# A two-layer decoder on one core: loading the tokens first, clearing the expert slots from another DMA queue, and writing out the first sequence's combination between the last shared groups

## The chip, the cores and the metric

The kernel runs on one core of a Trainium2 chip. A core has five engines, each with its own in-order instruction queue: TensorE (PE, matrix products and transposes[...]), VectorE (DVE), ScalarE (ACT), GpSimd (POOL) and SyncE (SP, which here only issues DMAs). [...] The metric is the device time of one execution in microseconds (us). Times of single instructions come from one profiled execution, and they are counted from the start of its span.

## What is computed

A decoder of two layers runs over 16 sequences of 256 tokens with 128 features, all in float32, with a context of 64 tokens of 96 features for each sequence. After each of six sublayers the input is added and the rows are normalised (post-norm). Cut to its frame, the reference is:

```python
x = _layernorm(x + _L0_attn_ref(x, ...))            # causal, 16 heads of 8
x = _layernorm(x + _L0_xattn_ref(x, ctx_768, ...))  # 8 heads of 16 on the context
x = _layernorm(x + _L0_ffn_ref(x, ...))             # 64 experts, top 6, and a shared FFN
x = _layernorm(x + _L1_attn_ref(x, ...))            # causal, 16 heads of 64
x = _layernorm(x + _L1_xattn_ref(x, ctx_768, ...))  # 16 heads of 64 on the context
x = _layernorm(x + _L1_ffn_ref(x, ...))             # attention whose tokens use 128, 64, 32 or 16 features
```

In the expert sublayer each token picks six of 64 experts by its softmax scores and a bias. An expert takes the first 64 tokens that picked it (tokens in order), each in a slot of its own; later ones are dropped. The expert and the shared FFN are both `silu(x w1) * (x w3)` times `w2`, with 88 hidden features in an expert and 176 in the shared FFN. A token's result is the sum of its experts' rows, each times its score, plus the shared FFN's row.

## The kernel before

**Recording and orders.** Most of the work is written as streams. A `Recorder` stands in for the engines: while a stream's function runs, calls are only stored, as units per engine. `interleaved` then takes an order, a long string written out ahead of time, in which each character names a stream and an engine, and emits the next unit of that stream on that engine:

```python
for c in order:
    b, e = divmod(LETTERS.index(c), len(ENGINES))
    for trace in waiting[b][e].pop(0):
        trace()
```

The sections under `manual_schedule` keep the emitted order on PE, DVE, ACT and POOL (`MANUAL`, L30). SP isn't in that set; the scheduler places SP's DMAs by when their buffers come free and what they depend on. Because all recorded calls pass through the helper at L141, nearly every row of the profile carries L141, and tile names tell the rows apart.

**Layer 0** (`ORDER0`, 17 streams). Stream 0, `contexts`, starts with `clear_slots` (L688 to 694): SP writes zeros over all 4096 slots of `xb` in DRAM (2 MB) and the spare row of `yb`. Then come the context's keys and values for layer 0 (`k0x`, `v0x`, from `ctxT`, `l0x_wk` and `l0x_wv`), and the products that fold layer 1's cross-attention into two tables in DRAM, `gd` and `hd`, one part for each head. The other 16 streams are `layer0(b)`, one for each sequence: load `x`, transpose it (`tp_x`), self-attention (tiles `..._0a`), norm, cross-attention (`..._0x`; the norm's inverse root `rs_0x` is a POOL instruction), norm into `x2` and, transposed, `x2T`, and the router. The router takes softmax scores (`sc`), adds the bias (`sb`), chooses six (`chosen`), counts slots with small products (`pos`), and gets each slot and each weight by comparing (`key`, `hit`). For each token tile and each of its six picks, POOL issues an indirect DMA that scatters 128 rows of `x2` into `xb`; there are 192 of these "puts".

**Experts** (program order). SP loads the weights of eight experts at a time (`e` tiles: `w1T`, `w3T`, `w2T`, 352 KB each, four groups in flight) and the constants of layer 1 (`l1_wqkv` 1.5 MB, `l1_wout`, and so on). The `e` tiles use memory that the pools of layer 0 release. `expert_tokens(g)` loads group g's 512 slots after all puts; PE transposes them (`xet`, `xeT`), then come the hidden products `eh`, `he`, the output `yp`, its copy `ye` on ACT, and SP's store to `yb`. The shared FFN runs in eight groups of 512 tokens: `shared_hidden(g)` makes `sh` on PE and `hs` on ACT and DVE, and `shared_out(g)` makes `z` on PE and adds it to `x2` on DVE. Groups 0 to 3 stand before the experts, groups 4 to 7 after them. `widths` prepares constants of the last sublayer in the middle of the experts.

**Layer 1** (`ORDER1`, 16 streams). First the pools of the experts are closed and new ones opened (`v1`, `vz`, `v2`); two tiles `vaf` are zeroed on POOL; and the value bias is folded into the output bias: DVE copies `bv`, PE multiplies it with `l1_wout` (`bv_out`), DVE adds the product to `l1_bout` (named `l_bout` in the profile; digits are left out of names). Each `layer1(b)` begins with 12 indirect DMAs on POOL that gather the tokens' expert rows `ge` from `yb`, and 12 DVE instructions that add them, weighted, to `x2` (`xr`). Then come norm (`st_0f`, `mv_0f`, `rs_0f`, result `x`), the transposed `x3T`, the products `qk` and `vp`, the output bias (`xpb_1a`, POOL), self-attention (`s_1a`, `nm_1a`, `p_1a`, `ptp_1a`), cross-attention with the tables `gx` and `hx` (loaded by SP from `gd` and `hd`), and the last sublayer.

## Time and profile before

| quantity | value |
|---|---|
| median of 3 runs (lowest to highest) | 1684.59 us (1684.14 to 1687.62) |
| the profiled execution's own time | 1679.19 us |
| span of the profiled execution | 1677.4 us |
| mean granted TensorE clock | 0.959 of full |
| busy PE, DVE, ACT, POOL | 1496.5, 1244.2, 1108.6, 830.6 us |
| DMA traffic | 73.89 MB, mean 44 GB/s |
| chain that ended last, by engine | PE 52%, DVE 24%, ACT 11%, issue 6%, POOL 4%, DMA 2% |

The profiled execution was about 5 us faster than the median; 1.8 us of its time lie around the span. A row of the profile gives a start, a duration, the engine, the operation, the tile written, the tiles read, their shapes and, in brackets, how long the engine had been idle and what ended that idle time. "SPq" is a DMA's issue in SyncE's queue, and not its transfer. The slices divide the span into 40 equal parts and give each engine's busy share in tenths.

By stage: layer 0 runs from 0 to about 626 us, the experts from 631.5 (first `eh`) to 668, the last shared groups and the transition to about 740, and layer 1 to the end.

### The profile page before, as it was taken

To read this page: it belongs to the slowest core of one execution; us is meant where nothing else is said; L and a number is where in the kernel's file an instruction comes from. 1 tells how busy PE (TensorE), PEld (TensorE's weight loads), DVE (VectorE), ACT (ScalarE), POOL (GpSimd) and SP (SyncE) were. 2 spreads that over 40 slices of the span, in tenths; PEclk is the share of its full clock that TensorE was granted. 3 is DMA by queue.
4 is the path that set the end of the run, shared out by engine and by line. 5 is a ranking of instruction groups with operands and counts; after the bars stand their busy time and mean duration, and the time that the engine had idled before them with its cause. 6 is when DMAs were issued, how large, how long until landed. Compare 5 with 4: busy or idle time off the path is not lost.

```text
span 1677.4 us, 36931 instructions
## 1 busy us (share of the span) xinstructions
PE 1496.5 (89%) x12738; PEld 1080.5 (64%) x12738; DVE 1244.2 (74%) x3788; ACT 1108.6 (66%) x3811; POOL 830.6 (50%) x910
## 2 busy tenths in 40 slices
PE   7989988889987679688998999998999999999996
PEld 4655555556554338466776877686777677777774
DVE  5788888879887643355778878777786787788675
ACT  4776777757776312155576777677676767786766
POOL 2144445444435440456727656664564576564441
PEclk9999999989999778789999999999999999999999
DMA  4111111111100066474202233222322333220000
GB/s 142 60 41 34 60 32 33 42 48 55 47 13 1 1 172 190 52 105 48 23 14 34 40 41 44 23 36 14 48 41 31 30 43 42 36 23 4 5 1 11
DMA packets 117190, 73.89 MB, mean 44 GB/s; under 512 B 46555, under 2 KB 106808, under 8 KB 116877
## 3 DMA queue, kind: packets, MB, share of 16 engines
q1 hardware_dynamic: 104717, 58.55, 12.8%
q0 software_dynamic: 12288, 13.00, 10.6%
q8 instruction: 102, 1.67, 0.4%
q14 instruction: 83, 0.68, 0.1%
HBM read 48.05 MB, written 35.65 MB: 50 GB/s over the span
## 4 chain that ended last, share of the span: by engine, by line
PE 52%; DVE 24%; ACT 11%; issue 6%; POOL 4%; DMA 2%; another core or an unknown queue 1%; SPq 0%; POOLq 0%; DVEq 0%; ACTq 0%
PE s_1a L141 5%; PE qk L141 4%; PE o_1a L141 4%; ACT p_0a L141 4%; PE ptp_1a L141 3%; PE s_0a L141 3%; PE ptp_1f L141 3%; PE vp L141 3%; PE pj_1x L141 3%; PE pj_1a L141 2%; PE ptp_0a L141 2%; DVE nm_0a L141 2%; PE s_1x L141 2%; ACT p_1a L141 2%; DVE x L141 2%
## 5 line engine op out<-in xcount | busy, mean ns | idle before, releaser
L141 POOL DMA_INDIRECT xb<-x,slots x192 | 189.1, 985 | 263.9 <-DVE hit L141 212.6
L141 POOL TENSOR_TENSOR p_1a<-p_1a,ri_1a 128x512 f32<-128x512 f32 x192 | 197.3, 1039 | 104.5 <-DVE ri_1a L141 89.3
L141 ACT ACTIVATE p_1a<-s_1a,nm_1a 128x256 f32<-128x256 f32 (+1 forms) x512 | 210.9, 445 | 50.5 <-DVE nm_1a L141 41.7
L141 ACT ACTIVATE p_0a<-s_0a,nm_0a 128x256 f32<-128x256 f32 (+1 forms) x512 | 211.5, 451 | 35.2 <-DVE nm_0a L141 33.6
L141 POOL DMA_INDIRECT ge<-yb,slots x192 | 195.7, 1019 | 54.4 <-issue 51.9
L141 ACT COPY pT_1a<-ptp_1a 128x512 f32<-128x512 f32 x192 | 106.1, 618 | 63.1 <-PE ptp_1a L141 55.1
L141 DVE TENSOR_REDUCE nm_1a<-s_1a 128x2 f32<-128x512 f32 (+1 forms) x192 | 126.1, 673 | 21.4 <-PE s_1a L141 21.3
L141 DVE TENSOR_REDUCE nm_0a<-s_0a 128x2 f32<-128x512 f32 (+1 forms) x192 | 125.0, 682 | 11.8 <-PE s_0a L141 10.5
L141 PE MATMUL qk<-x3T,l_wqkv 128*128 128x256 f32 x512 | 126.9, 390 | 2.7 <-issue 1.4
L141 ACT ACTIVATE p_1f<-s_1f,nm_1f 128x256 f32<-128x256 f32 x256 | 119.0, 499 | 10.4 <-DVE nm_1f L141 9.3
L141 PE MATMUL ptp_0a<-ident,p_0a 128*128 128x128 f32 x768 | 112.1, 281 | 13.5 <-ACT p_0a L141 7.9
L141 ACT COPY pT_0a<-ptp_0a 128x512 f32<-128x512 f32 x192 | 106.4, 615 | 23.7 <-PE ptp_0a L141 18.6
L141 ACT ACTIVATION_READ_ACCUMULATOR p_0a<-s_0a,nm_0a 128x1 f32 x512 | 120.8, 236 | 0.0
L141 ACT ACTIVATION_READ_ACCUMULATOR p_1a<-s_1a,nm_1a 128x1 f32 x512 | 117.9, 230 | 0.0
L141 PEld LDWEIGHTS qk<-x3T,l_wqkv 128*128 128x128 f32 x512 | 95.8, 197 | 20.1 <-issue 7.7
L141 PEld LDWEIGHTS ptp_0a<-ident,p_0a 128*128 128x128 f32 x768 | 86.4, 143 | 34.0 <-ACT p_0a L141 20.6
L141 PE MATMUL ptp_1a<-ident,p_1a 128*128 128x128 f32 x768 | 101.1, 275 | 7.7 <-POOL p_1a L141 3.9
L141 PE MATMUL s_1a<-kT,qT 64*128 64x256 f32 (+1 forms) x1024 | 104.4, 342 | 3.3 <-issue 2.3
L141 POOL TENSOR_TENSOR p_1x<-p_1x,cri_1x 128x512 f32<-128x512 f32 x64 | 65.9, 1044 | 66.6 <-DVE cri_1x L141 41.9
L141 PE MATMUL o_1a<-pT_1a,v 128*64 128x128 f32 x1536 | 95.4, 276 | 3.0 <-ACT p_1a L141 1.2
L141 PEld LDWEIGHTS s_1a<-kT,qT 64*128 64x128 f32 x1024 | 81.5, 192 | 23.3 <-issue 11.4
L141 DVE SCALAR_TENSOR_TENSOR xr<-ge,slot_w,xr 128x128 f32<-128x128 f32 x160 | 61.2, 383 | 46.8 <-DMA ge<-yb,slots 42.7
(258 smaller groups left out, 3710.9 us busy)
## 6 DMA issues: line engine op xcount, KB each, us to landing
gd<-g1x_sb SPq DMA_DIRECT2D x32, 256.0 KB
hd<-h1x_sb SPq DMA_DIRECT2D x32, 256.0 KB
gx<-gd SPq DMA_DIRECT2D x16, 512.0 KB
hx<-hd SPq DMA_DIRECT2D x32, 256.0 KB
xb<-x,slots POOLq DMA_INDIRECT x192
ge<-yb,slots POOLq DMA_INDIRECT x192
e<-in_w1T SPq DMA_DIRECT2D x8, 352.0 KB
e<-in_w3T SPq DMA_DIRECT2D x8, 352.0 KB
```

The lines of the kernel that those rows point to most:

```text
L141: r = f(*[made(x) for x in a], **{n: made(x) for n, x in k.items()})
```

## The change

Seven things are changed. Sizes, arithmetic and the number of heavy instructions stay as they are.

1. At the start, the tokens of sequence 0 and `l0_wqkv` are loaded first, then `ctxT`, `l0x_wk`, `l0x_wv`, then the rest of layer 0's weights, and the shared FFN's weights last. The two DMAs of `clear_slots` are issued by ScalarE, right after `l0_wqkv`.
2. The pool `fw` (scratch of the router and of the folded tables) is closed at the end of layer 0 and no longer after the experts.
3. `ORDER0` is rewritten. Compared engine by engine, the two orders differ in local swaps; in the last part more of the puts stand ahead of the last sequence's `rs_0x`.
4. `vaf` moves to the pool `wc` and is zeroed on DVE within `widths`; `v2` is opened early, on the right side of memory.
5. `gathered`, `combine`, `value_bias` and `add_value_bias` are functions of their own, and all that follows layer 0 lies in one manually scheduled section.
6. Between the last shared groups, the order is written out: the gathers of sequence 0 after `expert_out(7)`, the bias product before `shared_out(6)`, and the two halves of sequence 0's combination before and after `shared_out(7)`.
7. `ORDER1` is rewritten; stream 0 lacks its gathers and sums.

Where the built programs stand against each other, SP's order changes as well, although no line says so: the loads of `l1_bqkv`, `l1_wqkv` and `l1_wout` now come before the weights of the first four groups of experts, and the first `e` load waits for DVE's last `hit`; before, it waited for the last `sb`.

The diff, with the order strings cut to their first lines and the block that is only moved left out:

```diff
@@ -32,67 +32,67 @@
 
 LETTERS = "".join(chr(c) for c in range(35, 126) if chr(c) not in "\\")[: 17 * 5]
 ORDER0 = (
-    ',\'#\'#$#$+$#(#)($()*#*))$(*)*)()*))*())*)()*(*()*#*$#*#$**($**(#*)#$%(\'\'$%()\'\')(()*()*(1*)0-#.*((*-**.-(*..(*)#*'
...
+    '+\'#16;#$#$$(0#)$(()*#*))$*()*)()*))*())*)()*(*()*#*$#*#$**($**(#*)#$%(\'\'$%()\'\')(()*()*(*)-#@.*((*-**.-(*..(*)#'
...
 )
 ORDER1 = (
-    '&\'&$&$&&$&$$&$+,#$#+$)#%&#%+#$%$#$%)#%+#%#%#%$+$#%$$#$#)%+#$)#$$%)010$%$&.%+$#$&)%($&#)%$$(&%$%)+%($$&*$$&)#*('
...
+    '$\',16&+$#$#$+#%)#%&+#$%$#$%)#%+#%#%#%$+$#%$$#$#)%+#$)0#$0$%)%$$&.%+$#$&)%($&#)%$$(&%$%)+(%$$&#*($$*&%)(*0.#*(%'
...
 )
 
 
@@ -654,25 +654,38 @@
     phase_ab = ExitStack()
     xt_pool = pool_of(phase_ab, name="xt", bufs=1)
     x2T = xt_pool.tile([P, NT * P], F32, tag="x2T", name="x2T")
-    ctxT = load("ctxT", [DC, B, KV], pool=xt_pool)
-    fw = pool_of(phase_ab, name="fw", bufs=2)
-    ws1 = load("ws1T", [D, 2 * INTER], pool=xt_pool)
-    ws3 = load("ws3T", [D, 2 * INTER], pool=xt_pool)
-    ws2 = load("ws2T", [INTER, 2, D], pool=xt_pool)
 
     with ExitStack() as phase_a:
+        fw = pool_of(phase_a, name="fw", bufs=2)
         kx_pool = pool_of(phase_a, name="kx0", bufs=3)
         x0_pool = pool_of(phase_a, name="x0", bufs=1)
+
+        def tokens(b):
+            x = x0_pool.tile([P, 2, D], F32, tag="xin", bufs=3, name=f"x_{b}")
+            nc.sync.dma_start(x, a["x"][b * T : (b + 1) * T, :].rearrange("(i p) d -> p i d", p=P))
+            return x
+
+        tokens0 = tokens(0)
         l0_wqkv = load("l0_wqkvT", [D, 3 * D], pool=x0_pool)
+
+        nc.scalar.dma_start(
+            xb.rearrange("(s p) d -> p s d", p=P),
+            zero.unsqueeze(1).to_broadcast([P, NSLOT // P, D]),
+        )
+        nc.scalar.dma_start(yb[NSLOT : NSLOT + 1, :], zero[0:1, :])
+        ctxT = load("ctxT", [DC, B, KV], pool=xt_pool)
+        l0x_wk = load("l0x_wk", [DC, D], pool=x0_pool)
+        l0x_wv = load("l0x_wv", [DC, D], pool=x0_pool)
         l0_wout = load("l0_woutT", [D, D], pool=x0_pool)
         l0_bout = load_rows("l0_bout", x0_pool)
         l0x_wq = load("l0x_wq", [D, D], pool=x0_pool)
-        l0x_wk = load("l0x_wk", [DC, D], pool=x0_pool)
-        l0x_wv = load("l0x_wv", [DC, D], pool=x0_pool)
         l0x_wo = load("l0x_wo", [D, D], pool=x0_pool)
         l0x_bo = load_rows("l0x_bo", x0_pool)
         gate_w = load("gate_wT", [D, E], pool=x0_pool)
         gate_b = load_rows("gate_b", x0_pool)
+        ws1 = load("ws1T", [D, 2 * INTER], pool=xt_pool)
+        ws3 = load("ws3T", [D, 2 * INTER], pool=xt_pool)
+        ws2 = load("ws2T", [INTER, 2, D], pool=xt_pool)
         kT0x = x0_pool.tile([P, B * KV], F32, tag="kT0x", name="kT0x")
         vx0 = x0_pool.tile([P, B, 4, 2, 16], F32, tag="vx0", name="vx0")
         nc.gpsimd.memset(vx0, 0.0)
@@ -684,14 +697,6 @@
             (1, T, [[4 * t + j for j in range(2)] for t in range(4)]),
             (1, T, [[4 * t + j for j in range(2, 4)] for t in range(4)]),
         ]
-
-        def clear_slots():
-
-            nc.sync.dma_start(
-                xb.rearrange("(s p) d -> p s d", p=P),
-                zero.unsqueeze(1).to_broadcast([P, NSLOT // P, D]),
-            )
-            nc.sync.dma_start(yb[NSLOT : NSLOT + 1, :], zero[0:1, :])
 
         def context_keys_values():
             for g in range(2):
@@ -767,7 +772,6 @@
 
         def contexts():
 
-            clear_slots()
             context_keys_values()
             for c in range(8):
                 w = {}
@@ -797,8 +801,7 @@
 
         def layer0(b):
             nonlocal run
-            x = x0_pool.tile([P, 2, D], F32, tag="xin", bufs=3, name=f"x_{b}")
-            nc.sync.dma_start(x, a["x"][b * T : (b + 1) * T, :].rearrange("(i p) d -> p i d", p=P))
+            x = tokens(b) if b else tokens0
             xT = w2.tile([P, T], F32, tag="xT", name=f"xT_{b}")
             transposed(x, xT, f"x_{b}")
 
@@ -959,10 +962,13 @@
     f_ow = wc.tile([D, 4, D], F32, tag="f_ow", name="f_ow")
     f_ob = wc.tile([P, 2, D], F32, tag="f_ob", name="f_ob")
 
+    vaf = [wc.tile([P, 2, 8, 32], F32, tag=f"vaf_{i}", name=f"vaf_{i}") for i in range(2)]
+    v2 = pool_of(name="v2", bufs=2, side="right")
+
     def widths():
 
 
-        for t in (f_nb, f_mask, f_ow, f_ob):
+        for t in (f_nb, f_mask, f_ow, f_ob, *vaf):
             nc.vector.memset(t, 0.0)
         for e in range(4):
             m = D >> e
@@ -1048,61 +1054,13 @@
         rows = slice(g * G * CAP, (g + 1) * G * CAP)
         nc.sync.dma_start(yb[rows, :].rearrange("(i p) d -> p i d", p=P), ye)
 
-    with tc.manual_schedule(engines=MANUAL):
-
...
-        hs = shared_hidden(4)
-        expert_out(7, he)
-        shared(4, 8, hs)
-
-    phase_ab.close()
-
-
-    v1 = pool_of(name="v1", bufs=KB4_BUFS)
-    vz = pool_of(name="vz", bufs=1)
-    v2 = pool_of(name="v2", bufs=2)
-
-    vaf = [vz.tile([P, 2, 8, 32], F32, tag=f"vaf_{i}", name=f"vaf_{i}") for i in range(2)]
-    rounds1 = [(0, P, [[0, 2, 4, 6], [1, 3, 5, 7], [8, 10, 12, 14], [9, 11, 13, 15]])] + [
-        (1, T, [[h, h + 2], [h + 1, h + 3], [h + 4, h + 6], [h + 5, h + 7]]) for h in (0, 8)
-    ]
-    roundsf = [(qt, T, [[2 * t, 2 * t + 1] for t in range(4)]) for qt in range(2)]
-    for t in vaf:
-        nc.gpsimd.memset(t, 0.0)
-
-    bv = v1.tile([P, 8, P], F32, tag="kb4", name="bv")
-    bo = psum("bv_out")
-    with tc.manual_schedule(engines=MANUAL):
-        nc.vector.tensor_copy(bv, l1_bqkv[:, 16:24].unsqueeze(2).to_broadcast([P, 8, P]))
-        for c in range(8):
-            nc.tensor.matmul(bo[:, :D], bv[:, c, :], l1_wout[:, c, :], start=c == 0, stop=c == 7)
-        nc.vector.tensor_tensor(l1_bout, l1_bout, bo[:, :D], ALU.add)
-
-    def layer1(b):
-
-        ges = []
-        for i in range(2):
-            n = 2 * b + i
-            ge = v2.tile([P, TOPK, D], F32, tag="ge", name=f"ge_{n}")
-            ges.append(ge)
+    combined = {}
+    ges = {}
+
+    def gathered(b):
+
+        for n in (2 * b, 2 * b + 1):
+            ge = ges[n] = v2.tile([P, TOPK, D], F32, tag="ge", name=f"ge_{n}")
             for j in range(TOPK):
                 nc.gpsimd.indirect_dma_start(
                     out=ge[:, j, :],
@@ -1114,16 +1072,87 @@
                 )
                 if j % 2:
                     rec.unit()
-        r = v2.tile([P, 2, D], F32, tag="xr", name=f"xr_{b}")
-        for i in range(2):
+
+    def combine(b, halves=(0, 1)):
+        if 0 in halves:
+            combined[b] = v2.tile([P, 2, D], F32, tag="xr", name=f"xr_{b}")
+        r = combined[b]
+        for i in halves:
             n = 2 * b + i
+            ge = ges.pop(n)
             for j in range(TOPK):
                 nc.vector.scalar_tensor_tensor(
-                    r[:, i, :], ges[i][:, j, :], slot_w[:, n, j : j + 1],
+                    r[:, i, :], ge[:, j, :], slot_w[:, n, j : j + 1],
                     r[:, i, :] if j else x2[:, n, :], ALU.mult, ALU.add,
                 )
                 if j % 3 == 2:
                     rec.unit()
+        return r
+
+    def value_bias():
+
+        bv = [w3.tile([P, 4, P], F32, tag="p", bufs=P_BUFS, name=f"bv_{i}") for i in range(2)]
+        for i in range(2):
+            nc.vector.tensor_copy(bv[i], l1_bqkv[:, 16 + 4 * i : 20 + 4 * i].unsqueeze(2).to_broadcast([P, 4, P]))
+        return bv
+
+    def add_value_bias(bv):
+        bo = psum("bv_out")
+        for c in range(8):
+            nc.tensor.matmul(bo[:, :D], bv[c // 4][:, c % 4, :], l1_wout[:, c, :], start=c == 0, stop=c == 7)
+        nc.vector.tensor_tensor(l1_bout, l1_bout, bo[:, :D], ALU.add)
+
+    ctx.enter_context(tc.manual_schedule(engines=MANUAL))
+
...
+    hs4 = shared_hidden(4)
+    expert_out(7, he)
+
+    bv = value_bias()
+    gathered(0)
+    hs5 = shared_hidden(5)
+    shared_out(4, hs4)
+    hs6 = shared_hidden(6)
+    shared_out(5, hs5)
+    hs7 = shared_hidden(7)
+    add_value_bias(bv)
+    shared_out(6, hs6)
+    combine(0, (0,))
+    shared_out(7, hs7)
+    combine(0, (1,))
+
+    phase_ab.close()
+
+
+    v1 = pool_of(name="v1", bufs=KB4_BUFS)
+    rounds1 = [(0, P, [[0, 2, 4, 6], [1, 3, 5, 7], [8, 10, 12, 14], [9, 11, 13, 15]])] + [
+        (1, T, [[h, h + 2], [h + 1, h + 3], [h + 4, h + 6], [h + 5, h + 7]]) for h in (0, 8)
+    ]
+    roundsf = [(qt, T, [[2 * t, 2 * t + 1] for t in range(4)]) for qt in range(2)]
+
+    def layer1(b):
+        r = combined.pop(b, None)
+        if r is None:
+            gathered(b)
+            r = combine(b)
         x = w2.tile([P, 2, D], F32, tag="x", bufs=6, name=f"x3_{b}")
         layernorm(x, r, f"0f_{b}")
 
@@ -1230,8 +1259,7 @@
         layernorm(y, r, f"1f_{b}")
         nc.sync.dma_start(out[b * T : (b + 1) * T, :].rearrange("(i p) d -> p i d", p=P), y)
 
-    with tc.manual_schedule(engines=MANUAL):
-        interleaved(rec, [partial(layer1, b) for b in range(B)], ORDER1)
+    interleaved(rec, [partial(layer1, b) for b in range(B)], ORDER1)
```

## The prediction

> **What bounds the kernel now.** I read the page first (slices, then the chain), then the windows table of stages, then the timelines of TensorE (PE), VectorE (DVE) and SyncE's DMA queue (SPq) in the weak stretches, last the chain of waits there.
>
> The page's slices, each 41.9 us long:
>
> ```profile
> PE   7989988889987679688998999998999999999996
> ...
> PEclk9999999989999778789999999999999999999999
> DMA  4111111111100066474202233222322333220000
> ```
>
> TensorE is the bound nearly everywhere: 89% busy, mostly 9s. It is weak in the first slice and in slices 13 to 17 (545 to 755 us), where the granted clock drops as well. The windows table puts numbers on it (columns: window, its length, each engine's busy time with instruction count, granted clock, DMA share, GB/s):
>
> ```profile
> 540.00:600.00 60.00, 33.23 (x244) 18.96 (x244) 38.27 (x153) 19.39 (x63) 26.03 (x28) 0.72 0.01 1
> 600.00:631.00 31.00, 26.50 (x109) 14.31 (x109) 14.60 (x63) 5.51 (x9) 14.57 (x15) 0.84 0.88 250
> 631.00:668.00 37.00, 34.01 (x393) 31.98 (x393) 12.29 (x28) 8.25 (x14) 0.00 (x0) 0.91 0.68 192
> 668.00:742.00 74.00, 53.65 (x238) 35.02 (x237) 29.84 (x76) 18.26 (x54) 34.31 (x36) 0.78 0.63 89
> 742.00:1640.00 898.00, 849.39 (x7355) 665.27 (x7353) 692.70 (x1874) 644.28 (x2142) 530.99 (x568) 0.99 0.24 29
> ```
>
> PE idles 27 us in 540-600 (router's tail), 4.5 in 600-631, 3 in the experts, 20 in 668-742 (into layer 1). From 742 to 1640 it is 95% busy: time won before 742 stays won, and little can be won after it. The transition is where the change acts most. PE there:
>
> ```profile
> 688.33 0.39 PE L141 MATMUL z<-ws2T,hs 88*128 88x128 f32 x2
> 690.71 2.10 PE L141 MATMUL z<-ws2T,hs 88*128 88x128 f32 x14 [1.99 <-DVE xr L141]
> 699.96 0.80 PE L141 MATMUL z<-ws2T,hs 88*128 88x128 f32 x2 [7.14 <-DVE hs L141]
> 702.29 3.35 PE L141 MATMUL z<-ws2T,hs 88*128 88x128 f32 x14 [1.54 <-DVE hs L141]
> 707.13 3.76 PE L141 MATMUL bv_out<-l_wout,bv 128*128 128x128 f32 x16 [1.48 <-DVE bv L141]
> 710.67 0.64 PE L141 MATMUL tp_x<-ident,x 128*128 128x128 f32 x2
> ```
>
> The last shared groups' products z wait three times for VectorE, in whose in-order queue the shared units hs stand behind the sum xr of sequence 0's expert rows; and those wait for their gathers:
>
> ```profile
> 698.37 0.35 DVE L141 SCALAR_TENSOR_TENSOR xr<-ge,slot_w,xr 128x128 f32<-128x128 f32 x1 [0.84 <-DMA ge<-yb,slots]
> ...
> 701.05 0.60 DVE L141 TENSOR_SCALAR x<-xr,mv_0f,rs_0f 128x128 f32<-128x128 f32 x2 [0.85 <-POOL rs_0f L141]
> ```
>
> Sequence 0's normalised x exists at 701.65, yet tp_x takes it only at 710.67, behind z and bv_out: 9.0 us lost. GpSimd (POOL) loses time too, in the chain of waits:
>
> ```profile
> 706.27 4.98 issue
> 711.29 0.51 POOL xpb_1a L141
> ...
> 725.22 13.71 DMA ge<-yb,slots
> ```
>
> POOL's queue stood 5.0 us at xpb_1a for l_bout (the bias sum bv_out feeds), with sequence 1's and 2's gathers behind it; those then landed 13.7 us after their issue, beside the gx/hx loads. VectorE's nm_1a stood behind these sums, and PE behind that (PE's idle before tp_x at 740.81 is 2.75).
>
> **The start.** SyncE's queue in the profile of before:
>
> ```profile
> 8.32 5.53 SPq L141 DMA_DIRECT2D yb<-zero  x1
> ```
>
> The first PE instruction, k0x, starts at 7.20 and waits for l0x_wk, issued ninth at 4.59. The order afterwards is x, l0_wqkv, then (from ScalarE's queue) the 2 MB zero fill and yb's row, ctxT, l0x_wk. Issues cost 0.43 to 0.47 each, so l0x_wk is issued at about 0.8+3x0.45=2.2 instead of 4.6, behind 0.75 MB instead of 1.08 MB; but the fill now runs beside it. The rate then was 0.77 MB by 5 us. Without the fill k0x comes about 0.7 early. The Trainium skill, page "DMA: Bandwidth & Descriptors", section "Issuing engines are not separate DMA queues", speaks against the move: DMAs from different engines share the same 16 engines and interleave; a second issuer saves only issue time. By the rule, with half of the rate given to the fill until the first 0.75 MB is in, k0x would come up to 3 us late; by the row the SP block of 5.53 goes to ScalarE, whose queue has nothing due until 18.3 (it idled 16.2 us for kx), so that cover is wide. x's first waiting consumer (POOL's xpb_0a, 10.8) is not critical, and wk/wv/wqT/wo of the contexts come 5 us earlier than 13.89, not critical either. I take 0, bounds -0.7 and +3.
>
> **Layer 0's order.** The long order string is rewritten, but the two kernels' queues differ in local swaps only; no instruction is saved. I take 0, bounds -3 and +3 (over 16 sequences, VectorE-bound at 405 of 480 us in 60-540). The two tiles now cleared on VectorE among widths cost about 2x0.48 by the row of the same memset there; VectorE was busy 12.3 of 37 us in that window, so hidden: 0; without cover, 1.
>
> **The end of layer 0.** Two things. (1) The scatters (puts) of x2, 0.97 us every 1.28 us on POOL: 17 of the last ones stood behind rs_0x of sequence 15, now 12, so the last ends near 618.9 instead of 621.2: -2.3 if the expert-token load (issued 626.0) still hangs on it. (2) SyncE's order. Now l_wqkv (1.5 MB) and l_wout (0.5 MB) stand ahead of the experts' weights (4.2 MB), and the weights' memory comes free only with the last router hit (606.8; before, 600.7). Before:
>
> ```profile
> 611.80 0.33 SPq L141 DMA_DIRECT2D l_wqkv<-in_l_wqkv  x1
> ```
>
> While that moved, all engines stopped, though what they waited for was done:
>
> ```profile
> 623.69 0.69 DVE L141 TENSOR_TENSOR x<-z,x 128x512 f32<-128x512 f32 x1 [11.34 <-PE sh L141]
> ```
>
> (the z it reads ended at 613.35; TensorE then ran its queue dry, idle 1.84 at 619, followed by half clock). That transfer now goes at about 601 to 608. The stall may vanish (-3, its PE idle and half-clock loss), stay (0), or fall on the last hits and scatters: 11.3 us, less the slack of 4.8 (621.2 to 626.0) and the 2.3 above, is +4. The queue's total is the same 6.2 MB, ending near 624, so the weights are late for nobody (first used at 631.5). I take -2, bounds -5 and +4.
>
> **The transition.** PE's chain afterwards, from the end of the last sh at 688.3: bv_out is in the stream now and its bv copies are long done; 16 matmuls took 3.76 at half clock, so about 1.9 at full; then z of group 6 (2.2) and of 7 (2.2): done near 694, instead of 705.65. hs no longer stands behind xr. The first half of sequence 0's sum, 6x0.35=2.1, lies under z; the second half is bound by the gathers, whose issue is the same (678.4 to 693.7 on POOL) and whose last landing was 698.37. gx and hx of the first four sequences (4 MB) wait for the last z, so they now start at 694 instead of 705.7, beside the last three or four gathers. A gather landed every 1.55 us without them; at about 2.3 each with them, four cost 3 more: 701.4. Then bn, mv, rs_0f and x as before (3.3 us from last xr to x done, less 0.7 for the hs between them): x near 704, tp_x near 704.5: -6 (bounds: -9 without the collision, -4 with 703.5 as last landing).
>
> Sequence 1's gathers: POOL starts them after rs_0f, near 703 instead of 701.2, but without the 5.0 wait: last issue near 723 instead of 726.2; the loads, which filled the queue 706 to 741, are over by about 720 (4 MB at the 160 GB/s of that stretch is 25 us), so the landing lag shrinks from 13.7 towards the 5.6 of sequence 0. nm_1a and tp_x of sequence 1 should come 5 to 8 us earlier. Together I take -6.5, bounds -12 and +1.
>
> Here the skill's page "TensorE: Matmul & The Clock Gate", "What's actually happening", bears: full clock returns after about 3.4 us of sustained work. The trace disagrees: in the window 711-716 the clock was 0.50 with PE 4.39 of 5 us busy, 9 us after z had resumed. PE will still idle some 10 us (694 to 704) and so come back at half clock; by the rule the 9.2 us of qk would be half-cold, gaining some 2 us; by the row nothing. I take the row.
>
> **Layer 1's order.** Local swaps and one stream without its gathers: 0, bounds -3 and +3.
>
> **Sum.** 0+0-2-6.5+0 = -8.5. Profiled span 1677.4 gives 1668.9, with the 1.8 around it 1670.7; the median of the runs lies 5.4 above the profiled run's 1679.2, so 1676 for the median.
>
> **Rivals.** Gains and losses under 0.2% (3.4 us) can't be told from no change here.
> - *The gain is larger* (0.25): gathers don't feel gx/hx (x at 701), the 11 us stall vanishes, POOL's free queue is worth its 5 us: -5 and -10 = -15, 1669 or a little below. For it: the cause of each wait named is removed.
> - *As forecast* (0.43): 1672 to 1681.
> - *The gain is hidden* (0.15): the gathers decide everywhere. Sequence 0's last gather lands by 705, sequence 1's gathers, started later by as much, land when they did: -2 to -3, 1682. For it: PE waits through VectorE for ge already (42.7 us on the page's xr row).
> - *Slower* (0.17): the gx/hx loads starve sequence 0's gathers. They start at 694, 12 us earlier, and 25 us long. Lag was 13.7 us for gathers under such loads; the last gather of sequence 0 (issued 693) would land at 706.5, tp_x at 710, nothing gained; at a lag of 22 us, at 715, tp_x at 719: +8, with the -2 before it +6, 1691. It decides where the lag passes about 16 us. Against it: only four gathers are left in flight, while the lag of 13.7 was built up over a dozen. The added fill and stall bounds lie in this share too.
>
> Range 1666 to 1688: below is the sum's large-gain case with its tail, above the start of the slower case. Faster 0.68, same 0.15, slower 0.17.
>
> **What would show it.** Right: k0x at 6.5 to 8; z of group 7 done by 696, tp_x of sequence 0 at 701 to 706, no POOL wait for l_bout, xpb_1a at once; nm_1a of sequence 1 by 729; experts' eh near 629.5; the stretch after 742 keeping its length. Wrong: k0x after 10; x<-z or the last hits standing for 10 us inside the l_wqkv transfer; ge landing over 16 us after its issue near 693; layer 1's stretch (742 to the end) longer by what was won.

## The result and the profile after

The changed kernel is slower. Median 1693.80 us (1688.03 to 1699.45, 9 runs) against 1684.14 us before (1672.79 to 1687.62, 9 runs): the ratio is 1.0064, interval 1.0037 to 1.0090. A repeat, below, gave 1.0029 (1.0014 to 1.0045). The time lies above the range, and the sign of the forecast was wrong. The profiled execution took 1690.79 us (span 1689.0, clock 0.956), 11.6 more than that of before, and it is compared stage by stage here.

The page's slices after:

```profile
PE   7998989989987668768999999999998999999986
...
PEclk8999999999999769879999999999999999999999
DMA  3211110111200047474112232222313222230000
```

The weak slices, 12 to 17 (counted from 0), are still weak: no stage has become full. The windows of the same stages (length, busy PE, PEld, DVE, ACT and POOL, clock, DMA share, GB/s):

```profile
540.00:600.00 60.00, 37.97 (x306) 22.30 (x299) 41.11 (x168) 25.15 (x94) 28.91 (x31) 0.80 0.01 1
600.00:631.00 31.00, 20.70 (x78) 10.44 (x77) 12.83 (x67) 5.20 (x11) 13.57 (x15) 0.67 0.54 159
...
668.00:742.00 74.00, 58.31 (x350) 41.08 (x348) 24.73 (x56) 14.45 (x26) 28.65 (x29) 0.84 0.69 109
742.00:1640.00 898.00, 842.01 (x7302) 658.23 (x7301) 693.24 (x1869) 643.03 (x2146) 532.68 (x569) 0.98 0.25 30
```

A fixed window doesn't hold the same work in both kernels: the router's tail, whose last `pos` product started at 602.2 us, now reaches it at 615.0. So I followed single instructions and took the difference of their start times. The changed kernel is late by 2.0 us at `k0x`, 4.8 at the router of sequence 0 (86 us), 6.4 to 8.7 at the routers between 255 and 500, 12.8 at the last router product, 12.7 at the first `eh`, 13.8 at the last `yp`, 7.2 at `x3T` of sequence 0, 13.8 at `x3T` of sequence 1, and 11.6 at the end. **The loss is made before the experts. The transition wins 6.6 us back at sequence 0 and gives all of it away again one sequence later.** After that nothing systematic happens.

*The start.* SyncE's queue after (start, length of the issue), then PE's first instruction:

```profile
0.80 0.44 SPq L141 DMA_DIRECT2D x<-in_x  x1
...
2.38 1.13 SPq L141 DMA_DIRECT2D l0x_wk<-in_l0x_wk  x1
3.55 1.24 SPq L141 DMA_DIRECT2D l0x_wv<-in_l0x_wv  x1
```

```profile
9.16 3.75 PE L141 MATMUL k0x<-ctxT,l0x_wk 96*128 96x512 f32 x4 [9.16 <-DMA l0x_wk<-in_l0x_wk]
```

`l0x_wk` is issued at 2.38, as worked out, yet lands 6.8 us later (before, 2.6). From the moment ScalarE's fill runs, each issue on SyncE also takes 1.0 to 1.3 us and no longer 0.43.

*The end of layer 0.* VectorE's first `x<-z`, then TensorE, after:

```profile
631.52 0.69 DVE L141 TENSOR_TENSOR x<-z,x 128x512 f32<-128x512 f32 x1 [6.07 <-DMA xb<-x,slots]
```

```profile
642.59 0.66 PE L141 MATMUL xet<-ident,xe 128*128 128x128 f32 x4 [3.23 <-DMA xe<-xb]
...
644.19 4.92 PE L141 MATMUL eh<-xeT,e 128*88 128x64 f32 x32
```

The stall of `x<-z` shrank from 11.34 to 6.07 us, and the last `z` came 3.9 us earlier against the last `pos` product, but then PE ran out of work and waited for the expert tokens `xe`. SyncE issued that load at 638.78, 7.4 us after the issue of the last put (631.40); before, it was 5.8 (620.24 to 626.01). The new order of SyncE's loads, in which the weights follow 2 MB of layer 1's constants, makes the difference: with it the lag is 6.6 to 7.5 us in fifteen traces (7.2 in e3_fw below, which has nothing else new), and 5.7 to 6.3 in the five with the old one. How it does so isn't shown; that the puts land later beside more bulk data is a guess. The first `eh` then ran at half clock (granted clock 0.51 from 644 to 649 us; 4.92 us long, before 2.69).

*The transition.* TensorE, VectorE and GpSimd after:

```profile
703.93 3.19 PE L141 MATMUL z<-ws2T,hs 88*128 88x128 f32 x25
...
717.85 0.66 PE L141 MATMUL tp_x<-ident,x 128*128 128x128 f32 x2 [7.67 <-DVE x L141]
...
751.43 1.12 PE L141 MATMUL ptp_1a<-ident,p_1a 128*128 128x128 f32 x4 [6.39 <-POOL p_1a L141]
```

```profile
709.41 0.29 DVE L141 TENSOR_TENSOR l_bout<-l_bout,bv_out 128x128 f32<-128x128 f32 x1 [5.85 <-remote]
...
710.79 1.90 DVE L141 SCALAR_TENSOR_TENSOR xr<-ge,slot_w,xr 128x128 f32<-128x128 f32 x5
...
740.39 0.35 DVE L141 SCALAR_TENSOR_TENSOR xr<-ge,slot_w,xr 128x128 f32<-128x128 f32 x1 [2.63 <-DMA ge<-yb,slots]
...
747.49 0.35 DVE L141 SCALAR_TENSOR_TENSOR xr<-ge,slot_w,xr 128x128 f32<-128x128 f32 x1 [1.30 <-DMA ge<-yb,slots]
```

```profile
716.60 0.72 POOL L141 TENSOR_TENSOR rs_0f<-mv_0f,neg_half 128x2 f32<-128x2 f32 x1 [8.96 <-DVE mv_0f L141]
...
732.69 1.00 POOL L141 DMA_INDIRECT ge<-yb,slots  x1 [0.30 <-issue]
```

The last gather and the last sum of sequence 1 before:

```profile
721.31 1.00 POOL L141 DMA_INDIRECT ge<-yb,slots  x1 [0.31 <-issue]
```

```profile
733.53 0.35 DVE L141 SCALAR_TENSOR_TENSOR xr<-ge,slot_w,xr 128x128 f32<-128x128 f32 x1 [2.35 <-DMA ge<-yb,slots]
```

The three waits of `z` for `hs` are gone, and sequence 0's sums no longer wait for their gathers (five in a row take 1.90 us). They stand behind `l_bout` in VectorE's queue, which started 5.3 us after its product `bv_out` had ended (704.09).

Sequence 1 is best counted from the last `yp` (674.19 before, 687.99 after), since everything here starts 13.8 us later. Its gathers stand behind `rs_0f` on POOL, and that comes at 28.6 us after `yp`, before at 26.1. POOL's old wait of 5 us for `l_bout` is gone, so its last gather is issued at 44.7, 2.4 us earlier than before (47.1). But the last sum follows that issue by 14.8 us and no longer by 12.2, and so starts at 59.5 (before 59.3). Behind it in VectorE's queue stand `nm_1a`, then POOL's `p_1a`, then PE. The loads `gx` and `hx` fill SyncE's queue from 710.2 to 735.8, and data moved at 137 GB/s on average from 710.2 to 748: all of sequence 1's gathers lie beside them.

### The profile page after: what moved, and what is told of

It is laid out like the page before. It is cut to its first block, busy times and chain, and to the rows that moved or that the text cites. A ratio compares the mean times of both kernels' runs of the same rounds, so it can differ in the third digit from the quotient of the medians.

```text
span 1689.0 us, 36953 instructions
## 1 busy us (share of the span) xinstructions
PE 1498.0 (89%) x12738; PEld 1081.3 (64%) x12738; DVE 1247.0 (74%) x3791; ACT 1108.7 (66%) x3811; POOL 830.0 (49%) x908
## 4 chain that ended last, share of the span: by engine, by line
PE 52%; DVE 23%; ACT 10%; issue 6%; POOL 3%; DMA 3%; another core or an unknown queue 1%; SPq 0%; POOLq 0%; DVEq 0%; ACTq 0%
PE s_1a L141 5%; PE qk L141 5%; PE o_1a L141 4%; ACT p_0a L141 3%; PE ptp_1a L141 3%; PE s_0a L141 3%; PE ptp_1f L141 3%; PE pj_1x L141 2%; PE vp L141 2%; PE pj_1a L141 2%; PE ptp_0a L141 2%; DVE nm_0a L141 2%; PE s_1x L141 2%; DVE x L141 2%; ACT p_1f L141 2%
## 5 line engine op out<-in xcount | busy, mean ns | idle before, releaser
L141 PE MATMUL ptp_0a<-ident,p_0a 128*128 128x128 f32 x768 | 112.0, 282 | 12.7 <-ACT p_0a L141 6.4
```

Of the source, the lines that this page charges most:

```text
L141: r = f(*[made(x) for x in a], **{n: made(x) for n, x in k.items()})
```

## The experiments

Each row was timed in five rounds beside the kernel before on the same chip. Each kernel ran 6 to 22 times, the kernel before 15 to 75 times on each chip; its median there, in brackets, tells the chips apart. Besides the ratio with its 95% interval I give the difference of the means with its standard error, since the parts are compared by sums. "Start", "order" and "late half" name the three parts: the new start, the new `ORDER0`, and all else (early release of `fw`, `vaf`, the written-out end of the shared groups, `ORDER1`). My theory: the loss is in layer 0, by the start and the order; the late half gains little, because `gx` and `hx` hold up sequence 1's gathers. Rivals: the parts act on each other (the loss appears only together), or the late half loses.

### Which part costs what

Eight kernels, on two chips. The edits take the change's own hunks, one part at a time:

```diff
--- before          +++ e1_start        start only
--- before          +++ e2_order0       ORDER0 of after only
--- before          +++ e3_fw           this line only:
-    fw = pool_of(phase_ab, name="fw", bufs=2)
...
+        fw = pool_of(phase_a, name="fw", bufs=2)
--- after           +++ e4_late         start and ORDER0 of before
--- before          +++ e5_early        start and ORDER0 of after
--- after           +++ e6_old_order0   ORDER0 of before
--- after           +++ e7_old_start    start of before
--- after           +++ e8_after        the changed kernel again
```

> The kernel before with the new start alone (tokens first, the fill on ScalarE's queue, weights re-ordered; the old order string without the two units that went). Theory A, the loss is made at the start: the first product k0x at about 9.2 instead of 7.2, half clock for longer, sequence 0 about 5 us late at 60, and that persists: +4 to +7 us (ratio 1.003 to 1.004). Theory B, the loss is made by the rewritten order of layer 0: the start's 2 us are made up before 540, ratio 1.000 to 1.001. Theory C, the loss is made by the pool and SyncE's order: the same as B here.

> The kernel before with the new order string of layer 0 alone (the two units of the old start put back in front). Theory A: within 1.5 us of before. Theory B: +5 to +8 us, seen as a lag that grows between 60 and 600. Theory C: within 1.5 us.

> The kernel before with the pool fw closed after layer 0 alone, which also moves l_wqkv and l_wout ahead of the experts' weights in SyncE's queue. Theories A and B: within 1.5 us. Theory C: the experts' first eh 3 to 6 us later, because their weights and the scatters' data finish later: +3 to +6 us (ratio 1.002 to 1.0035).

> The changed kernel with the old start and the old order string of layer 0, so that only the late half of the change is left: the pool fw, vaf, the tail written out and the new order of layer 1. Theories A and B: what was forecast for the transition may show, -2 to -7 us against before. Theory C, or a transition whose gain is lost to sequence 1's gathers: 0 to +3 us against before.

> The kernel before with both early parts, the new start and the new order of layer 0, and nothing of the late half. The parts alone gave +1.5 and +1.5 us. Theory D, the parts add up: +3 us (ratio 1.002). Theory E, they work against each other (sequence 0 starts 2 us late against an order written for another start): +8 to +11 us, nearly the whole loss of the changed kernel.

> The changed kernel with the old order of layer 0 (without the two units that went), the rest as changed. Theory D: the sum of start and late half, within 1 us of before. Theory E: the same, since the pair is broken up. Theory F, the new start and the late half disturb each other: +6 us or more.

> The changed kernel with the old start (weights' order, fill on SyncE's queue), the rest as changed. Theory D: new order and late half, within 1.5 us of before. Theory E: the same. Theory G, the new order and the late half disturb each other: +6 us or more.

> The changed kernel as it is, run again beside the others. If the nine runs first measured are its true level: +10 us (ratio 1.006). If they were a high draw (the kernel before spreads over 19 us by itself): +1 to +6 us, which the three parts' +1.5, +1.5 and -2 would nearly explain.

| kernel | median us (before) | ratio, interval | difference of means, us |
|---|---|---|---|
| e1_start | 1684.82 (1683.19) | 1.0009, 0.9987 to 1.0031 | +2.3 ± 1.4 |
| e2_order0 | 1686.32 (1683.19) | 1.0009, 0.9992 to 1.0027 | +3.2 ± 1.2 |
| e3_fw | 1681.77 (1683.19) | 0.9991, 0.9975 to 1.0007 | −1.0 ± 1.0 |
| e4_late | 1680.75 (1683.19) | 0.9988, 0.9974 to 1.0002 | −1.9 ± 0.9 |
| e5_early | 1687.94 (1681.38) | 1.0025, 1.0007 to 1.0044 | +5.3 ± 1.3 |
| e6_old_order0 | 1681.49 (1681.38) | 0.9995, 0.9982 to 1.0007 | −0.3 ± 0.8 |
| e7_old_start | 1685.81 (1681.38) | 1.0028, 1.0014 to 1.0043 | +4.4 ± 1.1 |
| e8_after | 1688.42 (1681.38) | 1.0029, 1.0014 to 1.0045 | +5.7 ± 1.1 |

The order costs +3.2 alone, +3.0 (e5 less e1), +6.3 (e7 less e4) and +6.0 (e8 less e6): about +4.6 ± 0.7. The start costs +2.3, +2.1, +1.6 and +1.3: about +1.8 ± 0.7. The late half gives −1.9, −2.6, +1.2 and +0.4: about −0.7 ± 0.7, of 8.5 us forecast. Together that is +5.7, as e8 has it; but three quarters of that sum is e8 itself, so it is no second proof. Nor do the parts surely add up. The order costs 3.1 without the late half and 6.1 with it, or, put the other way, the late half gains 2.2 with the old order and loses 0.8 with the new one. That difference, 3.0 ± 1.4, is about twice its standard error, so the rival that the parts act on each other isn't excluded. The early release of `fw` by itself does nothing measurable. It can't be taken out of the late half: without it the early `v2` doesn't fit in memory. `ORDER1` wasn't tried by itself.

The start is seen at `k0x`: 7.0 to 7.6 us in the kernels with the old start, 9.2 to 9.6 with the new one.

### Where in the order the loss sits

Hybrids of the two strings: the prefix of one up to a cut, then the remaining letters in the order of the other. The cut lies after 5/6 of the string (about 495 us). g3 cuts later, in the middle of sequence 13's attention. `g0_base`, the control of the g kernels, is `d1_late_delay` of the next section.

```diff
--- e4_late         +++ h1_old_head_new_tail    before's string, then after's order from 5/6 on
--- e4_late         +++ h2_new_head_old_tail    after's string, then before's order from 5/6 on
--- d1_late_delay   +++ g0_base                 nothing
--- d1_late_delay   +++ g1_all_new              after's string
--- d1_late_delay   +++ g2_new_tail             before's string, then after's order from 5/6 on
--- d1_late_delay   +++ g3_new_end              the same with the later cut
```

> Old start, late half as changed (the base that gave 1680.8), and in layer 0 the old order for the first five sixths and the new one from there (some 495 us on). Theory H, the new order's loss lies in its rewritten tail (sequences 13 to 15): lg of sequence 11 to lg of sequence 14 takes 103.5 to 105 us instead of 100, the way from the last pos to the first eh is 3.5 us shorter, sum +1 to +2. Theory I, it lies in the head (sequence 5 above all, near 250 us): the tail alone gains, -1 to +0.5 us against the base.

> The same base with the new order for the first five sixths and the old one from there. Theory H: within 1 us of the base (1680.8). Theory I: lg of sequence 3 to lg of sequence 5 takes 73.5 us instead of 71.8, +2.5 to +4.5 us against the base.

> The control for the next three: old start, late half as changed, gx and hx delayed behind sequence 2's gathers, old order of layer 0. Both theories: 0.995 of before (8 us less).

> The control with the new order of layer 0. Both theories: 4 to 5 us over the control.

> The control with the new order from five sixths of layer 0 on. Theory H2, head and tail each lose some 2 us: 1.5 to 3 us over the control, lg of sequence 12 to lg of sequence 14 4 us longer, from there to the first eh 2 to 3 us shorter. Theory I2, the head loses all: within 1 us of the control.

> The control with the new order only from the middle of sequence 13's attention on (about 525 us). If the forecast gain of the last scatters is real and the loss lies before that point: lg of sequence 12 to lg of sequence 14 as in the control, from there to the first eh 2 to 3 us shorter, 1 to 3 us under the control. If the loss lies in the same stretch as the gain: 1 to 3 us over the control, as in the run before.

| kernel | median us (before) | ratio, interval | difference of means, us |
|---|---|---|---|
| h1_old_head_new_tail | 1658.77 (1657.74) | 0.9999, 0.9984 to 1.0015 | −0.3 ± 1.1 |
| h2_new_head_old_tail | 1658.41 (1657.74) | 0.9998, 0.9979 to 1.0016 | −1.4 ± 1.4 |
| g0_base | 1683.21 (1689.64) | 0.9962, 0.9943 to 0.9981 | −5.8 ± 1.2 |
| g1_all_new | 1688.56 (1689.64) | 0.9996, 0.9973 to 1.0018 | −1.0 ± 1.8 |
| g2_new_tail | 1682.09 (1689.64) | 0.9961, 0.9945 to 0.9978 | −6.8 ± 1.3 |
| g3_new_end | 1687.63 (1689.64) | 0.9992, 0.9973 to 1.0011 | −1.7 ± 1.4 |

On the chip of h1 and h2 neither half told itself apart from before (their base, e4, wasn't run there). On the other chip the order costs +4.8 ± 2.0 (g1 less g0), and its last sixth costs nothing (g2 less g0: −1.0 ± 1.6). By these two the loss sits in the first five sixths, where the strings differ least. That went against my reading of the first trace, which shows 5 us lost between the routers of sequences 12 and 14: those 5 are lost in g2 as well (75.5 us against 70.6 in g0) and 3.8 of them come back before the first `eh` (63.4 against 67.2), and the whole of g2 is no slower than g0. g3 should have kept only the gain; it lost 4.1 ± 1.6 against g0 (77.5 in the same stretch). Its changed end is part of g2's, so the two don't fit together unless a hybrid is an order of its own, and that holds for g2 too. The place of the loss is likely and not shown.

In the head, the stretch from the router of sequence 3 to that of sequence 5 takes 73.3 to 75.5 us in six traces with the new order and 70.0 to 71.9 in ten with the old (the chip of h1 and h2 left out, where both lie between 69.6 and 73.4). One place in it shows what the difference is made of. VectorE in the changed kernel (e8), then in the same with the old order (e6):

```profile
251.76 0.23 DVE L141 COPY va<-vp 128x64 f32<-128x64 f32 x1 [3.36 <-remote]
```

```profile
250.05 0.23 DVE L140 COPY va<-vp 128x64 f32<-128x64 f32 x1 [1.58 <-PE vp L140]
```

The queues differ only in that two `hit`s stand ahead of `va` on VectorE with the new order and behind it with the old. With the old order VectorE goes on when PE's `vp` ends (250.01); with the new one PE's `vp` ends at 249.54, and VectorE stands 2.2 us longer, released by nothing the profile can name. The chain of waits of e8 says it so:

```profile
248.40 3.34 another core or an unknown queue
...
559.88 3.50 another core or an unknown queue
```

Within the first 620 us, such pieces in the chain come to 6.8 us in e8, 8.1 in e2, 8.1 in e5, 6.9 in e7 and 12.0 in g1 (all with the new order, all with one near 244 to 252; the first trace of the changed kernel has only the later one, 3.6), and to 0 to 2.7 in the old-order kernels before, e1, e3, e4, e6 and g0. What they are isn't settled. Packets of the two instruction-load queues lie within some 3 us of many of them, but lie near the same place in e4, which has no stall there, and last no longer (1.0 to 1.2 us for 16 KB, by the median) in kernels without stalls. g2 has long ones too (8.4 us in the first 620) and loses nothing. So: the order costs about 4.6 us, most likely in its first five sixths, and unexplained waits at a few places go along with it. That these waits are its cause isn't shown.

### The gathers and the loads beside them

The late half with one thing more: the `gx` and `hx` loads of sequences 0 to 3 wait until sequence 2's gathers have landed. In `ORDER1` their SyncE letters move behind these gathers. `gx` is first used at 803.7 us in e8, over 90 us after its load, so there is room.

```diff
+    gets = []
+    def later(b, load):
+        if b < 4:
+            for get in gets:
+                tc.add_manual_dep(load.ins, get.ins.name, landed, reason="behind the gathers")
...
+                    then=gets.append if b == 2 else None,
...
-        nc.sync.dma_start(gx, gd[:, :, b * KV : (b + 1) * KV].rearrange("h p k -> p h k"))
+        nc.sync.dma_start(gx, gd[:, :, b * KV : (b + 1) * KV].rearrange("h p k -> p h k"), then=partial(later, b))
...
+                then=partial(later, b),
```

`d1_late_delay` is e4 with it, `d2_before_delay` the kernel before with it and nothing else. `f1_fill_last_delay` is the changed kernel with before's `ORDER0`, the delay, and the zero fill issued by SyncE behind all of layer 0's weights; `f2_best` is f1 again, beside d2:

```diff
-        nc.scalar.dma_start(
+        nc.sync.dma_start(
             xb.rearrange("(s p) d -> p s d", p=P),
```

> The base with one more edit: the gx and hx loads of sequences 0 to 3 (4 MB, first used at some 803 us) wait for the gathers of sequence 2. If the gain of the written-out tail is lost because these loads run beside sequence 1's gathers: its gathers land 1.4 us apart, x3T of sequence 0 to x3T of sequence 1 takes 28 to 30 us instead of 35.5, and the time is 5 to 7 us under the base (near 1675). If the gathers' own pace decides (12 of them at 1.3 us, started 7 us earlier or not), that way stays at 33 to 36 us and the time within 2 us of the base.

> The changed kernel with the old order of layer 0, the fill issued by SyncE behind all weights instead of by ScalarE ahead of ctxT, and gx and hx delayed as in the run before. If the fill beside the first loads is what delays the first product: k0x at 5 to 6 us instead of 9.7 to 10.3, and 2 us under the old start's 7.2 to 7.9. The time is then that of the run before it less 1 to 2 us, near 1673 to 1674. If the order of the loads decides: k0x stays over 7.

> The kernel before with one edit: the gx and hx loads of sequences 0 to 3 wait for sequence 2's gathers. If the tail and the delay are each half of one gain: x3T of sequence 0 at the old 37 us behind the last yp, and x3T of sequence 1 earlier by some 2 to 4 us (its gathers land without the loads beside them): -2 to -4 us against before. If the loads were never in the old tail's way: within 1.5 us. If the delay alone gives everything: -7 us, as much as the run with both.

> New order of the loads with the fill behind the weights, old order of layer 0, written-out tail, gx and hx delayed, beside the run before on one chip: 0.994 to 0.996 of before (7 to 10 us less), x3T of sequence 0 to x3T of sequence 1 30 us.

| kernel | median us (before) | ratio, interval | difference of means, us |
|---|---|---|---|
| d1_late_delay | 1650.91 (1657.74) | 0.9949, 0.9931 to 0.9966 | −9.0 ± 1.2 |
| f1_fill_last_delay | 1649.08 (1657.74) | 0.9940, 0.9919 to 0.9960 | −10.5 ± 1.6 |
| d2_before_delay | 1678.53 (1687.72) | 0.9951, 0.9931 to 0.9971 | −8.3 ± 1.7 |
| f2_best | 1674.21 (1687.72) | 0.9913, 0.9889 to 0.9937 | −13.8 ± 1.8 |

The traces say what each piece does (us between the same two instructions):

| kernel | last `yp` to `x3T` of sequence 0 | on to `x3T` of sequence 1 | both |
|---|---|---|---|
| before | 37.2 | 30.2 | 67.4 |
| after | 30.6 | 36.7 | 67.3 |
| d2_before_delay | 37.6 | 25.0 | 62.6 |
| f2_best | 30.5 | 30.3 | 60.8 |

The written-out end brings sequence 0 forward by 6.6 us. Without the delay, sequence 1 takes back 6.5 of it. The delay brings sequence 1 forward by 4.8 us in the kernel before (67.4 to 62.6) and by 6.5 with the written-out end (67.3 to 60.8). So the loads do hold up these gathers. But they are not where the 6.6 us went: with the loads out of the way, sequence 1 still takes back 5.3 of 7.1, and the written-out end is worth 1.8 us there (60.8 against 62.6; g0 has 60.6). The rest was never won, since the gathers themselves are issued little earlier: the last of sequence 1 at 44.7 us after the last `yp` in f2_best, at 47.5 in d2. The rows: SyncE's first `gx` in f2_best, and VectorE's last sum of sequence 1 in f2_best and in d2.

```profile
759.34 0.00 SPq L139 DMA_DIRECT2D gx<-gd  x1
```

```profile
728.29 0.35 DVE L139 SCALAR_TENSOR_TENSOR xr<-ge,slot_w,xr 128x128 f32<-128x128 f32 x1 [1.46 <-DMA ge<-yb,slots]
```

```profile
729.28 0.35 DVE L140 SCALAR_TENSOR_TENSOR xr<-ge,slot_w,xr 128x128 f32<-128x128 f32 x1 [1.42 <-DMA ge<-yb,slots]
```

Behind the issue of its gather that sum comes after 8.5 us in f2_best and 7.4 in d2, instead of 14.8 in the changed kernel and 12.2 before. The delay alone gives the kernel before 8.3 us (difference of means), more than the 4.8 of the table: it also removes the loads from beside sequence 2's gathers (`x3T` of sequence 1 to that of sequence 2: 32.7 against 36.4). That is about what d1 and g0, which have the late half as well, gain on other chips (9.0 and 5.8). f2_best is 5.5 ± 1.8 better than d2; the traces account for 1.8 of that here and for about 0.6 at `k0x`, and the two profiled spans differ by only 0.8 us (1670.0 and 1670.8), so how much the written-out end and the fill at the back add to the delay stays open. f2_best's `l0x_wk` and `k0x`:

```profile
2.26 0.43 SPq L139 DMA_DIRECT2D l0x_wk<-in_l0x_wk  x1
...
8.94 5.14 SPq L139 DMA_DIRECT2D yb<-zero  x1
```

```profile
6.51 3.75 PE L139 MATMUL k0x<-ctxT,l0x_wk 96*128 96x512 f32 x4 [6.51 <-DMA l0x_wk<-in_l0x_wk]
```

With nearly the same issue time and no fill beside it, `l0x_wk` lands 2.7 us earlier than in the changed kernel, and each issue takes 0.43 again. f2_best beats both kernels and has the lowest ratio of all that were run.

## Why the prediction was wrong

Between the forecast (−8.5) and the repeat (+5.7) lie 14.2 us: 7.8 are the late half, 4.6 the order, 1.8 the start.

- **The start (0, bounds −0.7 and +3): the rule that spoke against it was right, and the size lay within the bounds.** As the Trainium skill has it (page "DMA: Bandwidth & Descriptors", section "Issuing engines are not separate DMA queues"), a second issuer gave no second share of the engines: `k0x` came about 2 us late and the time rose by about 1.8. The queue's issue time was worked out rightly (2.2, measured 2.38); that the issues after it stretch to over 1 us beside the fill was not foreseen. That `k0x` comes 0.7 early without the fill was right: 6.51 in f2_best, against 7.20. I weighed ScalarE's idle cover, which was never the question. Taking 0 between −0.7 and +3 meant taking neither of the two sides I had argued.
- **Layer 0's order (0, bounds −3 and +3, "the two kernels' queues differ in local swaps only; no instruction is saved"): this step failed, and with the start it makes the sign.** It costs about +4.6. That no instruction is saved says nothing about waits between engines, and "local" was no reason for zero. Nor is the last part local: in the last sixth about half of VectorE's units stand at another place, which cost 5 us at the routers of sequences 12 to 14 in the trace and gave most of it back. "VectorE-bound" was a misreading as well: from 60 to 540 us PE was busy 427.8 us, VectorE 405.4. The bound was too narrow. Why the order costs this is open.
- **`widths` on VectorE (0): no cost of it is seen.** It wasn't tried by itself; the late half as a whole has none to show.
- **The end of layer 0 (−2): the gain came smaller and was eaten, and the stall was put down to the wrong thing.** From the last `pos` product to the issue of the last put it takes 16.44 us after and 18.08 before, 1.6 less where 2.3 was forecast: of the twelve puts left behind `rs_0x`, the first waits 8.74 us for a `hit`. The `xe` load then follows 7.4 us after the last put's issue and no longer 5.8. The stall of `x<-z` had nothing to do with the transfer of `l_wqkv`. In e3_fw that transfer is issued at 605.66, and `x<-z` still stands, from 617 to 628:

```profile
628.22 0.69 DVE L141 TENSOR_TENSOR x<-z,x 128x512 f32<-128x512 f32 x1 [11.25 <-PE z L141]
```

  Nor had "all engines stopped": POOL issued a put every 1.28 us throughout, and PE ran until 619. The stall is 10.6 to 11.9 us in all eight traces with the old end of the order, 4.6 to 9.1 in the eight with the new one, and 1.03 in all four on the chip of f1. What it is stays open.
- **The transition (−6.5): the first half right in number and partly by luck, the second half failed.** At sequence 0: −6.6 measured, −6 forecast. But the forecast took the last sums to wait for gathers beside `gx` and `hx`; they waited for nothing of the kind, and stood behind `l_bout`, which the profile gives no releaser. On the chip of f1, where `l_bout` waits 1.03 us, `x3T` of sequence 0 comes 28.2 to 29.0 us after the last `yp` instead of 30.6. "Sequence 1's gathers … nm_1a and tp_x of sequence 1 should come 5 to 8 us earlier": they came no earlier at all. The issue of the gathers gained 2.4 us, about as forecast (3). The failed term is the lag, "from 13.7 towards the 5.6 of sequence 0": it grew from 12.2 to 14.8 (the 13.7 and the 726.2 of the prediction belong to a gather of sequence 2). I had the loads over by about 720; with the shift of 13.8 taken off they were issued until 722.0 and moved data until about 734, and sequence 1's gathers, at 703.7 to 718.9, lay under all of it. Even by the forecast's own times, 694 to 720 for the loads and 703 to 723 for the gathers, the lag could not shrink. Without the loads the lag is 8.5, and sequence 1 comes 6.6 us earlier than before (f2_best). That is the rival "the gain is hidden", in its second half.
- **The clock (nothing gained at `qk`): right in effect, by a wrong reading.** The window 711 to 716 ends where the clock returns: it is 0.50 from 712 to 716 and 1.00 from 716 to 721, 4.1 us after `qk` began (711.92). After, it is 0.50 from 719 to 722.6 and 1.00 from 722.6 to 728, 3.5 us after `qk` began (719.12). That fits the rule which the prediction set aside. `qk` took 8.86 us instead of 9.16, as its first part ran at half clock both times.
- **Layer 1's order (0): no loss seen.** From `x3T` of sequence 1 to the end it is 935.9 us before and 933.7 after; the other kernels with before's `ORDER1` and no delay take 934.0 to 938.1.
- **The rival "slower" (gathers of sequence 0 starved) did not happen**: sequence 0's sums run without a wait for `ge` (1.90 us for five in a row). The time came out slower all the same, by the order and the start, which this rival named only as a bound ("the added fill") or not at all.

The first comparison, at +9.7 between medians, lies higher than the repeat (+5.7 ± 1.1); the two intervals overlap, and what the other 4 us were isn't shown.

## What to carry to other kernels

Work brought forward is won only if the next consumer's data comes forward too: write down for the step *after* the one you move what it will wait for, where its own requests stand in their queue, and what moves beside them. A prefetch with 90 us of room that ran beside small gathers cost more here than a whole rearrangement of the code gained; delaying it gave 0.5% to the unchanged kernel. And an edit that only reorders a hand-written order between engines isn't free until it is measured: here it cost 4.6 us, more than the bound of 3.

## What the runs showed of the hardware that I had not expected

- Beside a 2 MB fill issued by ScalarE, the *issues* in SyncE's queue took 1.0 to 1.3 us instead of 0.43, and `l0x_wk` landed 6.8 us after its issue instead of 4.3 (f2_best).
- Waits that the profile puts down to nothing on the core ("remote") depend on the chip. The bias sum `l_bout` waits for PE's `bv_out` in the same place of one and the same kernel; here f2_best, and then f1, which is the same code on another chip:

```profile
696.42 0.29 DVE L139 TENSOR_TENSOR l_bout<-l_bout,bv_out 128x128 f32<-128x128 f32 x1 [5.83 <-remote]
```

```profile
685.83 0.29 DVE L139 TENSOR_TENSOR l_bout<-l_bout,bv_out 128x128 f32<-128x128 f32 x1 [1.03 <-PE bv_out L139]
```

  In all ten traces of the written-out end on other chips it is 4.5 to 6.4 us and "remote"; in all four traces on the chip of f1 it is 1.03. Those four have no such piece in their chain, where all others have 4.3 to 35.7 us of them. On that chip the kernel before has a median of 1657.74 us, elsewhere 1681 to 1690. Whether these waits are what makes the difference, and what they are, stays open; the one trial that would bear on it, the whole new order on that chip, wasn't made.
- Single runs of one program on one core spread with a standard deviation of about 5 us (before, nine runs: 1672.79 to 1687.62), so that an effect of 2 us needs the sums of several kernels, as above.
